# A two-layer transformer block on one Trainium2 core: the context's 192 features contracted as 128 rows and a rest of 64

## The chip, the core and the metric

The kernel is one program on one core of a Trainium2 chip. The core has five engines that run side by side and wait for each other through semaphores: TensorE (PE; its weight loads are listed apart as PEld), VectorE (DVE), ScalarE (ACT), GpSimd (POOL) and SyncE (SP), which here issues nearly all DMA transfers. TensorE's products land in PSUM, 128 partitions by eight banks of 512 fp32 columns; VectorE and ScalarE read them from there. The metric is the device time of one execution in microseconds, lower is better.

## What is computed

Two layers, each of self-attention, cross-attention to a context, and a gated feed-forward part, with a layer norm ahead of each and everything in fp32. x is (4, 512, 320): four batches of 512 tokens. The context is (4, 1601, 192). There are 20 heads of 16.

```python
def _attn(x, ctx, wq, wk, wv, wo, bo, heads):
    q = (x @ wq).reshape(b, n, heads, dh).transpose(0, 2, 1, 3)
    k = (ctx @ wk).reshape(b, j, heads, dh).transpose(0, 2, 1, 3)
    v = (ctx @ wv).reshape(b, j, heads, dh).transpose(0, 2, 1, 3)
    sim = jnp.einsum('bhid,bhjd->bhij', q, k) * scale
    a = jax.nn.softmax(sim, axis=-1)
    out = jnp.einsum('bhij,bhjd->bhid', a, v)
    return out.transpose(0, 2, 1, 3).reshape(b, n, heads * dh) @ wo + bo
...
x = _attn(h1, h1, q1, k1, v1, o1_w, o1_b, heads) + x
x = _attn(h2, context, q2, k2, v2, o2_w, o2_b, heads) + x
ff = a * jax.nn.gelu(g, approximate=False) @ ff_w2 + ff_b2
```

The change touches `ctx @ wk` and `ctx @ wv` of cross-attention: 192 features contracted, 1601 tokens, 320 columns, in each layer and batch.

## The kernel before

The program is a list of units. An attention unit is one layer, kind, batch and group of four heads (five groups, so 20 self-attention and 20 cross-attention units a layer); a feed-forward unit is one batch. The context's tokens are cut into 13 chunks of 128 (the last has 65).

**Rounds.** A cross unit runs 13 rounds, one for each chunk. In a round TensorE makes the scores of four heads (`st`, L1300: key times query in two parts, plus the row of maxima `nrows`), and beside them products of a coming unit from which its row maxima are taken (`sps`, L1068, and L1095 for the last 65 tokens). These run on four tiles of 32 rows by 128 columns. ScalarE turns `st` into exponentials `pr` (L1310), VectorE takes the maxima of `sps` (L1083). Then TensorE multiplies the exponentials of the chunk before with the values (`av`, L1326, tiles of 128 rows by 32 columns); ScalarE copies `av` out (L1345) and GpSimd adds it up (L1346). A self unit has 4 rounds of the same kind.

**Steps.** All other TensorE work of the attention stages is cut into steps that the scheduler puts between an `av` and the next round's scores: queries (`qps`, L941), output projections (`ops`, L1226), keys of the context (`kps`, L965, function `keys_of_context`) and values (`vps`, L1029, function `add_values`). Each step has an estimated cost and a due round; a credit that grows with the work still to be done says whether a round gets no step, one or more. The order is fixed when the program is built. A step takes a PSUM bank (of eight, chosen by the time at which each is expected to be free), writes it and has it copied out by VectorE or ScalarE, whichever is expected to be free first (`taken`, L1008 and L1011).

**The two steps that change.** The transposed context lies in a tile `[96, 2, tokens]`: 192 features as two times 96 partitions. A value step makes one chunk of 128 tokens for eight heads (128 columns) or twelve (192 columns): two contractions of 96 rows, each on four tiles of 128x32, one for each 32 tokens. There are 13 such steps for each of the two head sets. A key step makes 200 or 201 tokens of each half of the tokens for one unit, again in two contractions of 96 rows on four tiles; four steps make a unit's keys. Then GpSimd splits the keys into a high and a low part (`split`, L817 and L818), and SP moves them to the unit's key buffer `kT` (L866). Each fp32 product stands as two records in the trace.

**The context.** In layer 0, VectorE transposes it in blocks of 32, SP saves it to DRAM (L755), and loads it for each batch and layer in four bands for each of the two times 96 features (L769).

## Time and profile before

| what | time |
|---|---|
| three runs, median | 2946.81 us |
| three runs, lowest and highest | 2944.68 and 2947.46 us |
| the profiled execution's span | 2948.5 us |
| TensorE busy in it | 2871.7 us |
| VectorE busy | 2060.2 us |
| ScalarE busy | 1890.3 us |
| GpSimd busy | 1287.7 us |
| kps products, 2560 records (L965) | 330 to 541 ns each |
| vps products of cross-attention, 3264 records (L1029) | 270 to 350 ns each |

The profiled execution is a fourth one, with its own span. In the timeline a line has the start and the length in us, the engine, the source line, the operation, the tile written and those read, the shape, and how many instructions were merged; square brackets hold the idle time ahead of it and what ended it. A record's length is longer than the time after which the next one can begin, since products overlap; starts are the better measure. Group lines give busy time and the mean of one after the bar.

### The profile page before, as it was taken

What the parts mean: (1) busy time and instruction counts of PE and PEld (TensorE: products, weight loads), DVE (VectorE), ACT (ScalarE), POOL (GpSimd) and SP (SyncE); (2) the same over time, 40 slices, a digit from 0 to 9 for tenths busy, and PEclk for the clock granted to TensorE, in tenths of its full rate; (3) what the DMA queues carried; (4) which work ended last, traced back from release to release, by engine and by line L of the source; (5) the groups of instructions that cost most, each with busy time, mean ns of one, the idle gap of its engine ahead of it and who ended that gap; (6) DMA issues with size and microseconds to landing.
All of it is one profiled execution on the core that took longest, in us unless ns stands there. A gap on an engine that the chain in (4) does not pass through costs nothing.

```text
span 2948.5 us, 84388 instructions
## 1 busy us (share of the span) xinstructions
PE 2871.7 (97%) x35018; PEld 1513.0 (51%) x35018; DVE 2060.2 (70%) x4031; ACT 1890.3 (64%) x3754; POOL 1287.7 (44%) x1409
## 2 busy tenths in 40 slices
PE   8999999999999999999999999999999999999999
PEld 4555555555555554355554555555555555544554
DVE  7777888888888878323258678888888888873221
ACT  3867677887877878501138676778778788783000
POOL 3556345545545545211225563455455464451110
PEclk8999999999999999999999999999999999999999
DMA  4444224232232112200113342222221121222000
GB/s 106 107 124 101 69 67 108 52 89 59 50 93 68 47 50 62 83 18 11 42 40 89 100 101 68 64 62 54 54 65 47 50 72 45 58 53 78 20 22 14
DMA packets 186543, 188.70 MB, mean 64 GB/s; under 512 B 69668, under 2 KB 137264, under 8 KB 186160
## 3 DMA queue, kind: packets, MB, share of 16 engines
q1 hardware_dynamic: 185368, 182.11, 24.4%
q8 instruction: 276, 4.52, 0.6%
q10 hardware_dynamic: 760, 1.18, 0.2%
q14 instruction: 107, 0.88, 0.1%
q0 software_dynamic: 32, 0.00, 0.0%
HBM read 55.76 MB, written 29.36 MB: 29 GB/s over the span
## 4 chain that ended last, share of the span: by engine, by line
PE 81%; DVE 13%; ACT 1%; DMA 1%; issue 1%; POOL 1%; SPq 1%; POOLq 0%; ACTq 0%; DVEq 0%
PE av L1326 22%; PE st L1300 16%; PE fps L1411 10%; DVE pm L1083 8%; PE sps L1068 6%; PE yps L1518 6%; PE vps L1029 5%; PE ops L1226 3%; PE kps L965 3%; PE qkps L900 3%; DVE nmax L1083 3%; PE fps L1471 2%; PE qps L941 2%; PE sps L1095 1%; ACT pr L1310 1%
## 5 line engine op out<-in xcount | busy, mean ns | idle before, releaser
L1310 ACT ACTIVATE pr<-st 128x512 f32<-128x512 f32 (+1 forms) x2720 | 1404.4, 604 | 399.8 <-PE st L1300 364.9
L1083 DVE TENSOR_REDUCE pm<-sps 128x1 f32<-128x512 f32 x1920 | 1188.0, 681 | 147.7 <-PE sps L1068 139.0
L1346 POOL TENSOR_TENSOR o<-o,vo 128x512 f32<-128x512 f32 x576 | 739.2, 1283 | 960.8 <-ACT vo L1345 937.5
L1068 PE MATMUL sps<-kT,q 32*128 32x512 f32 x4800 | 867.5, 430 | 10.6 <-DMA q<-low 3.4
L1300 PE MATMUL st<-q,kT 32*128 32x512 f32 (+1 forms) x5120 | 782.4, 420 | 2.2 <-ACT low L916 1.7
L1326 PE MATMUL av<-pr,vals 128*32 128x512 f32 (+1 forms) x5440 | 736.8, 607 | 45.5 <-ACT pr L1310 10.0
L1300 PEld LDWEIGHTS st<-q,kT 32*128 32x128 f32 (+1 forms) x5120 | 417.2, 180 | 290.4 <-issue 120.4
L1300 PE MATMUL st<-nrows,ones 32*128 32x512 f32 (+1 forms) x2720 | 539.1, 399 | 9.4 <-DMA nrows<-turned 9.4
L1068 PEld LDWEIGHTS sps<-kT,q 32*128 32x128 f32 x4800 | 425.6, 184 | 91.1 <-ACT pr L1310 13.4
L1083 DVE TENSOR_REDUCE nmax<-sps 128x1 f32<-128x512 f32 x640 | 396.3, 681 | 103.6 <-PE sps L1068 96.0
L1345 ACT COPY vo<-av 128x512 f32<-128x512 f32 x576 | 354.1, 615 | 23.9 <-PE av L1326 20.1
L1482 ACT ACTIVATE gl<-fps,b 128x512 f32<-128x512 f32 x80 | 54.6, 687 | 414.4 <-PE fps L1471 303.2
L1411 PE MATMUL fps<-hT,w 128*128 128x512 f32 x640 | 283.0, 597 | 0.0
L1326 PEld LDWEIGHTS av<-pr,vals 128*32 128x32 f32 (+1 forms) x5440 | 111.1, 108 | 320.4 <-DVE pm L1083 182.1
L1300 PEld LDWEIGHTS st<-nrows,ones 32*128 32x128 f32 (+1 forms) x2720 | 245.1, 180 | 34.4 <-issue 8.4
L1483 DVE SCALAR_TENSOR_TENSOR hid<-fps,b,gl 128x512 f32<-128x512 f32 x80 | 59.6, 748 | 241.1 <-ACT gl L1482 239.1
L1411 PEld LDWEIGHTS fps<-hT,w 128*128 128x128 f32 x640 | 119.3, 190 | 155.3 <-issue 152.1
L1518 PE MATMUL yps<-w,hid 128*128 128x320 f32 x640 | 176.3, 435 | 0.1
L1518 PEld LDWEIGHTS yps<-w,hid 128*128 128x128 f32 x640 | 120.4, 190 | 56.5 <-ACT gl L1482 4.5
L1226 PEld LDWEIGHTS ops<-wo,aT 112*32 112x32 f32 (+1 forms) x3072 | 97.9, 110 | 57.9 <-issue 41.2
L1226 PE MATMUL ops<-wo,aT 112*32 112x160 f32 (+1 forms) x3072 | 124.1, 300 | 0.7 <-POOL aT L1208 0.6
L517 POOL TENSOR_SCALAR root<-root 128x4 f32<-128x4 f32 x22 | 5.2, 237 | 263.9 <-DVE root L511 263.2
(91 smaller groups left out, 2493.1 us busy)
## 6 DMA issues: line engine op xcount, KB each, us to landing
kT<-stages SPq DMA_DIRECT2D x160, 200.2 KB
oway<-o SPq DMA_DIRECT2D x80, 256.0 KB
q<-high SPq DMA_DIRECT2D x160, 64.0 KB
q<-low SPq DMA_DIRECT2D x160, 64.0 KB
kT<-high SPq DMA_DIRECT2D x60, 128.0 KB
q<-high SPq DMA_DIRECT2D x60, 128.0 KB
kT<-low SPq DMA_DIRECT2D x57, 128.0 KB
aT<-oway SPq DMA_DIRECT2D x32, 224.0 KB
```

What stands on the lines that cost most here:

```text
L900: nc.tensor.matmul(ps[f : f + m, :w], lhsT=wqk[:n, k, f // GD, column : column + m], rhs=first.hT[:n, k, at : at + w], start=(k == 0), sto ...
L1029: nc.tensor.matmul(ps[f : f + m, :w], lhsT=u.kvT[:n, k, at + f : at + f + m], rhs=wv[:n, k, h0 * DH : h1 * DH], start=(k == 0), stop=(k == ...
L1068: nc.tensor.matmul(ps, lhsT=u.q[j * SLOT : (j + 1) * SLOT, e, t * P : (t + 1) * P], rhs=u.kT[j * SLOT : (j + 1) * SLOT, u.k0 + s * 512 : u ...
L1083: nc.vector.tensor_reduce(to[:, j : j + 1], ps, AX.X, ALU.max)
L1226: nc.tensor.matmul(ps[f : f + m, : D // 2], lhsT=aT[:n, k, f * NQ + t * SLOT : f * NQ + t * SLOT + m], rhs=wo[:n, k, cols], start=(k == 0) ...
L1300: nc.tensor.matmul(own[0][:r, :], lhsT=ones[rows, :r] if e == 2 else u.keys(rows, c), rhs=u.rows[rows, :] if e == 2 else u.q[rows, e, :], ...
L1310: nc.scalar.activation(p[:r], own[0][:r], AF.Exp)
L1326: nc.tensor.matmul(ps[j * SLOT : (j + 1) * SLOT, :], lhsT=columns_of[:r, head : head + SLOT], rhs=pr.pop((c, j))[:r, :], start=True, stop= ...
L1345: nc.scalar.copy(vo, ps)
L1346: nc.gpsimd.tensor_tensor(u.o, u.o, vo, ALU.add)
L1411: nc.tensor.matmul(ps, lhsT=w1[:, k, i * FF + c * P : i * FF + (c + 1) * P], rhs=natural(u.hT[:, k]), start=start, stop=stop,)
L1518: nc.tensor.matmul(ps[:, :D], lhsT=hid[c][:, t * P : (t + 1) * P], rhs=w2[:, c, :], start=(c == 0), stop=(c == NHC - 1),)
```

## The change

Features 0 to 127 become one contraction of 128 rows; the remaining 64 a second one. Two such rests, of different tokens, lie side by side in one tile: one on partitions 0 to 63, the other on 64 to 127 (`RESTS`; the weights' rest is loaded twice, once for each half). A value step now makes two chunks that are three apart (`PAIRS`; the thirteenth alone) into two banks: main rows of the one, main rows of the other, then both rests on tiles of 64x32. A key step makes two cuts of the tokens into two banks in the same way, so two steps make a unit's keys. The token halves become 768 and 834 long; 66 tokens' products are made twice so that both halves of a bank have one width. The high part of the keys moves into the tile `w1`. The context's last 65 tokens are saved apart, and the context is loaded in five bands for the main rows and five for the rests. Estimated costs and due rounds of the steps follow. What follows the products (copies, split, moves) is otherwise the same.

```diff
 DK = [(0, 0, 112), (1, 112, 112), (2, 224, 96)]
 HK = [(0, 0, P), (1, P, 96), (2, P + 96, 96)]
-CK = [(0, 0, 96), (1, 96, 96)]
...
 KB = CTX // 32
-RUN = NC2 * 32
+KM = P // 32
+CR = CTX - P
 TOK = S2 + 1
-HALF = TOK // 2
-WIDTHS = [RUN - 32 + max(0, min(32, S2 - (NC2 - 1) * P - 32 * i)) for i in range(4)]
-WIDTHS[3] += TOK - S2
-BANDS = [(sum(WIDTHS[:i]), w) for i, w in enumerate(WIDTHS)]
+RUN = (NC2 - 1) * 32
+TAIL = TOK - 4 * RUN
+HALF = 2 * RUN
+LONG = HALF + TAIL
+
+
+RESTS = [(0, 0), (CR, 0), (0, RUN), (CR, RUN), (CR, 2 * RUN)]
+CROSS_W = TOK + RUN * 2 + TAIL
+QC = RUN // P
+PAIRS = [(c, c + QC) for h in range(2) for c in range(2 * h * QC, (2 * h + 1) * QC)] + [(NC2 - 1,)]
+STEP_OF = {c: i for i, pair in enumerate(PAIRS) for c in pair}
 KW = NC2 * P
 NHC = FF // P
...
-KCUT = slices(HALF, 4)
+KCUT = list(zip(slices(RUN, 2), ((RUN, RUN // 2), (RUN + RUN // 2, RUN // 2 + TAIL))))
...
-        room["low"], room["high"] = part(HALF), part(HALF)
+        room["low"] = part(LONG)
+        room["high"] = w1_flat[:, 2 * D + CROSS_W : 2 * D + CROSS_W + LONG]
...
         room["context"] = [
-            w1_flat[:96, 2 * D : 2 * D + 2 * TOK].rearrange("p (k w) -> p k w", k=2),
-            one.tile([96, 2, TOK], F32, tag="ctxT", name="ctxT"),
+            (t[:, :TOK], t[:, TOK:])
+            for t in (w1_flat[:, 2 * D : 2 * D + CROSS_W], one.tile([P, CROSS_W], F32, tag="ctxT", name="ctxT"))
...
-                lambda k=k: dma(out=t[:96, k], in_=w[k * 96 : (k + 1) * 96, :].rearrange("(k d) c -> d k c", d=32))
-                for k in range(2)
+                lambda k=k, to=to, at=at, n=n: dma(
+                    out=t[to : to + n, k], in_=w[at : at + n, :].rearrange("(k d) c -> d k c", d=32)
+                )
+                for k, to, at, n in ((0, 0, 0, P), (1, 0, P, CR), (1, CR, P, CR))
...
-            dma(out=saved[b][:, :, c0 * 32 : (c0 + n) * 32], in_=s[i][:, :, : n * 32])
+            if c0 + n < NC2:
+                dma(out=saved[b][:, :, c0 * 32 : (c0 + n) * 32], in_=s[i][:, :, : n * 32])
...
+            for band in range((TAIL + 31) // 32):
+                w = min(32, TAIL - band * 32)
+                dma(out=tails[b][:, :, band * 32 : band * 32 + w], in_=s[i][band * 32 : (band + 1) * 32, :, :w])
...
-            for i, (at, w) in enumerate(BANDS):
-                dma(
-                    out=s["cT"][:, k, at : at + w],
-                    in_=saved[b][i * 32 : (i + 1) * 32, k * 3 : (k + 1) * 3, :w],
-                )
+            main, rest = s["cT"]
+            for i, (row, col) in enumerate(RESTS):
+                part = saved[b][i * 32 : (i + 1) * 32] if i < 4 else tails[b]
+                w = RUN if i < 4 else TAIL
+                if k == 0:
+                    dma(out=main[:, i * RUN : i * RUN + w], in_=part[:, :KM])
+                else:
+                    dma(out=rest[row : row + CR, col : col + w], in_=part[:, KM:])
...
         def keys_of_context(part):
 
-            at, w = KCUT[part]
-            ps = bank("kps")
-            written(0.1 + w * 4 * 2 / 2400, ps)
-            for k in range(2):
+            cuts = KCUT[part]
+            main, rest = first.kvT
+            pss = [bank("kps") for _ in cuts]
+            written(0.2 + (sum(w for _, w in cuts) + cuts[1][1]) * 4 / 2400, *pss)
+            for e, (at, w) in enumerate(cuts):
                 for i in range(2):
                     for f in range(GT):
                         nc.tensor.matmul(
-                            ps[(i * GT + f) * SLOT : (i * GT + f + 1) * SLOT, :w],
-                            lhsT=wk2[:, k, u.g * GD + f * SLOT : u.g * GD + (f + 1) * SLOT],
-                            rhs=first.kvT[:, k, i * HALF + at : i * HALF + at + w],
-                            start=(k == 0),
-                            stop=(k == 1),
+                            pss[e][(i * GT + f) * SLOT : (i * GT + f + 1) * SLOT, :w],
+                            lhsT=wk2[:, 0, u.g * GD + f * SLOT : u.g * GD + (f + 1) * SLOT],
+                            rhs=main[:, i * HALF + at : i * HALF + at + w],
+                            start=True,
+                            stop=False,
+                        )
+            for i in range(2):
+                for f in range(GT):
+                    for e, (at, w) in enumerate(cuts):
+                        rows = slice(e * CR, (e + 1) * CR)
+                        col = (i - e) * RUN + at
+                        nc.tensor.matmul(
+                            pss[e][(i * GT + f) * SLOT : (i * GT + f + 1) * SLOT, :w],
+                            lhsT=wk2[rows, 1, u.g * GD + f * SLOT : u.g * GD + (f + 1) * SLOT],
+                            rhs=rest[rows, col : col + w],
+                            start=False,
+                            stop=True,
                         )
             low, high = room["low"], room["high"]
-            taken(low[:, at : at + w], ps[:, :w], ps, 0.12 + w * 0.001)
+            for (at, w), ps in zip(cuts, pss):
+                taken(low[:, at : at + w], ps[:, :w], ps, 0.12 + w * 0.001)
             if part + 1 < len(KCUT):
                 return
             split(low, high)
 
             def half(i):
-                to = u.kT[:, i * HALF : (i + 1) * HALF]
-                return [(to[h::2], t[i * GD : (i + 1) * GD]) for h, t in enumerate((high, low))]
+                w = (HALF, LONG)[i]
+                to = u.kT[:, i * HALF : i * HALF + w]
+                return [(to[h::2], t[i * GD : (i + 1) * GD, :w]) for h, t in enumerate((high, low))]
...
-            for part, (_, w) in enumerate(KCUT):
+            for part, cuts in enumerate(KCUT):
                 add(
-                    chain, 0.05 + w * 8 / 2400, lambda part=part: keys_of_context(part),
-                    keys_due - 2 * (len(KCUT) - 1 - part), lambda part=part: part or keys_free(),
+                    chain, 0.15 + (sum(w for _, w in cuts) + cuts[1][1]) * 4 / 2400, lambda part=part: keys_of_context(part),
+                    keys_due - 4 * (len(KCUT) - 1 - part), lambda part=part: part or keys_free(),
                 )
...
+        def cross_values(i, step):
+
+            h0, h1 = PARTS[i]
+            w = (h1 - h0) * DH
+            cols = slice(h0 * DH, h1 * DH)
+            main, rest = u.kvT
+            chunks = PAIRS[step]
+            pss = [bank("vps") for _ in chunks]
+            written(0.2 + w * 4 * (1 + len(chunks)) / 2400, *pss)
+            for c, ps in zip(chunks, pss):
+                for f, m in tiles_of(u.row_count(c)):
+                    nc.tensor.matmul(
+                        ps[f : f + m, :w],
+                        lhsT=main[:, c * P + f : c * P + f + m],
+                        rhs=wv2[:, 0, cols],
+                        start=True,
+                        stop=False,
+                    )
+            for f, m in tiles_of(u.row_count(chunks[0])):
+                for c, ps in zip(chunks, pss):
+                    b = c // QC if c < NC2 - 1 else 4
+                    row, col = RESTS[b]
+                    at = col + (c % QC if b < 4 else 0) * P + f
+                    rows = slice(row, row + CR)
+                    nc.tensor.matmul(
+                        ps[f : f + m, :w],
+                        lhsT=rest[rows, at : at + m],
+                        rhs=wv2[rows, 1, cols],
+                        start=False,
+                        stop=True,
+                    )
+            for c, ps in zip(chunks, pss):
+                put(i, c, ps)
             u.vmade[i] += 1
...
-            for c in range(u.nch):
-                add(
-                    "values", 0.05 + w / 600 * len(parts_k), lambda i=i, c=c: values(i, c),
-                    units[u.i + g].start + 2 * c, lambda c=c, free=free: free(c),
-                )
+            for c in range(u.nv):
+                if u.cross:
+                    add(
+                        "values", 0.15 + w / 600 * (1 + len(PAIRS[c])), lambda i=i, c=c: cross_values(i, c),
+                        units[u.i + g].start + 2 * PAIRS[c][0], lambda c=c, free=free: free(PAIRS[c][-1]),
+                    )
+                else:
+                    add(
+                        "values", 0.05 + w / 600 * len(HK), lambda i=i, c=c: values(i, c),
+                        units[u.i + g].start + 2 * c, lambda c=c, free=free: free(c),
+                    )
...
-                until(lambda: units[u.i - u.g].vmade[u.g // 2] > c, "values")
+                until(lambda: units[u.i - u.g].vmade[u.g // 2] > (STEP_OF[c] if u.cross else c), "values")
```

Where the steps stand on TensorE. First a value step in the first layer's second batch, heads 0 to 7 (`vps`; `av` ends the round before, `nrows` and `ones` the scores before that). Before:

```order
L1300 MATMUL st<-nrows_98,ones 128x512 x2
L1068 MATMUL sps<-kT_134,q_102 128x512 x2
L1326 MATMUL av<-pr,vals 32x512 x4
L1029 MATMUL vps<-wv_115,ctxT 32x128 x8
L1300 MATMUL st<-q_104,kT_135 128x512 x2
```

With the change, one round without a step and the step behind it, from behind an `av`:

```order
L1381 MATMUL st<-q_104,kT_139 128x512 x2
L1149 MATMUL sps<-kT_138,q_102 128x512 x2
L1381 MATMUL st<-q_104,kT_139 128x512 x2
L1149 MATMUL sps<-kT_138,q_102 128x512 x2
L1381 MATMUL st<-nrows_98,ones 128x512 x2
L1381 MATMUL st<-q_104,kT_139 128x512 x4
L1149 MATMUL sps<-kT_138,q_102 128x512 x2
L1381 MATMUL st<-nrows_98,ones 128x512 x2
L1149 MATMUL sps<-kT_138,q_102 128x512 x2
L1407 MATMUL av<-pr,vals 32x512 x4
L1090 MATMUL vps<-wv_115,ctxT 32x128 x8
L1103 MATMUL vps<-wv_115,ctxT 32x128 x8
```

Eight products in one round became sixteen in every second round (L1090 the main rows, L1103 the rests); the round ahead, which held a step of its own, has none. Next a key step in the same layer's last batch, before:

```order
L1068 MATMUL sps<-kT_135,q_104 128x512 x2
L1326 MATMUL av<-pr,vals 32x512 x4
L965 MATMUL kps<-ctxT,w_116 32x200 x8
L1300 MATMUL st<-q_103,kT_101 128x512 x2
L1068 MATMUL sps<-kT_135,q_104 128x512 x2
```

With the change, the second of the unit's two key steps in the same round:

```order
L1407 MATMUL av<-pr,vals 32x512 x4
L989 MATMUL kps<-ctxT,w_116 32x192 x4
L989 MATMUL kps<-ctxT,w_116 32x258 x4
L1001 MATMUL kps<-ctxT,w_116 32x192
L1001 MATMUL kps<-ctxT,w_116 32x258
L1001 MATMUL kps<-ctxT,w_116 32x192
L1001 MATMUL kps<-ctxT,w_116 32x258
L1001 MATMUL kps<-ctxT,w_116 32x192
L1001 MATMUL kps<-ctxT,w_116 32x258
L1001 MATMUL kps<-ctxT,w_116 32x192
L1001 MATMUL kps<-ctxT,w_116 32x258
L1381 MATMUL st<-q_103,kT_101 128x512 x2
```

The step holds the main rows of both cuts (L989), then the rests in turn from the two row halves (L1001).

More of the change, by code (lines that the diff above doesn't have):

```diff
@@ L732 @@
     saved = [dram.tile([P, KB, RUN], F32, name=f"ctxT{b}") for b in range(B)]
+    tails = [dram.tile([32, KB, TAIL], F32, name=f"tail{b}") for b in range(B)]
     users = []
@@ L1014, in add_values, with put @@
     def add_values(u):
-        parts_k = CK if u.cross else HK
-        wv = wv2 if u.cross else wv1
+        def put(i, c, ps):
+            h0, h1 = PARTS[i]
+            w = (h1 - h0) * DH
+            r = u.row_count(c)
+            taken(vals[:r, c, h0:h1, 0:DH], ps[:r, :w].rearrange("p (h d) -> p h d", d=DH), ps, 0.12 + w * 0.001)
         def values(i, c):
```

27 lines of the change are left out of this document (17 added, 10 removed).

## The prediction

> **What bounds the kernel now.** I read the page's shares and chain first, then the busy time in stretches, then the operations of the two tiles that change, then single rounds in the timeline of TensorE.
>
> ```profile
> span 2948.5 us, 84388 instructions
> PE 2871.7 (97%) x35018; PEld 1513.0 (51%) x35018; DVE 2060.2 (70%) x4031; ACT 1890.3 (64%) x3754; POOL 1287.7 (44%) x1409
> PE 81%; DVE 13%; ACT 1%; DMA 1%; issue 1%; POOL 1%; SPq 1%; POOLq 0%; ACTq 0%; DVEq 0%
> PE av L1326 22%; PE st L1300 16%; PE fps L1411 10%; DVE pm L1083 8%; PE sps L1068 6%; PE yps L1518 6%; PE vps L1029 5%; PE ops L1226 3%; PE kps L965 3%; PE qkps L900 3%; DVE nmax L1083 3%; PE fps L1471 2%; PE qps L941 2%; PE sps L1095 1%; ACT pr L1310 1%
> ```
>
> TensorE is busy for 97% and holds 81% of the chain; VectorE's maxima (L1083) are the only other entry of weight. The two operations that change, vps and kps, hold 5% and 3%. The stretches of the two cross-attention stages, columns PE, PEld, DVE, ACT, POOL, granted clock, DMA:
>
> ```profile
> 430.00:1190.00 760.00, 740.66 (x10571) 393.45 (x10574) 637.42 (x1237) 611.11 (x1228) 401.29 (x389) 1.00 0.27 67
> 1888.00:2646.00 758.00, 738.52 (x10620) 391.29 (x10612) 631.94 (x1205) 612.66 (x1228) 402.21 (x389) 1.00 0.23 56
> ```
>
> There VectorE works 84% of the time (637.42 of 760) and ScalarE 80%: TensorE binds, with two engines close behind. How close shows in one window that holds three kinds of round (TensorE alone; a round runs from one av to the next):
>
> ```profile
> 745.15 1.07 PE L1326 MATMUL av<-pr,vals 128*32 128x512 f32 x8
> 746.04 1.48 PE L941 MATMUL qps<-hT,wq 128*32 128x256 f32 x24
> 748.97 1.06 PE L1326 MATMUL av<-pr,vals 128*32 128x512 f32 x8
> ...
> 751.70 1.07 PE L1326 MATMUL av<-pr,vals 128*32 128x512 f32 x8
> ...
> 754.23 1.06 PE L1326 MATMUL av<-pr,vals 128*32 128x512 f32 x8
> 755.11 0.87 PE L965 MATMUL kps<-w 96*32 96x201 f32 x16
> ...
> 757.44 1.06 PE L1326 MATMUL av<-pr,vals 128*32 128x512 f32 x8
> ```
>
> and another with a value step and a round without a step before it:
>
> ```profile
> 606.85 1.07 PE L1326 MATMUL av<-pr,vals 128*32 128x512 f32 x8
> ...
> 609.61 1.06 PE L1326 MATMUL av<-pr,vals 128*32 128x512 f32 x8
> 610.50 0.62 PE L1029 MATMUL vps<-wv,ctxT 96*32 96x128 f32 x16
> ...
> 612.58 1.06 PE L1326 MATMUL av<-pr,vals 128*32 128x512 f32 x8
> ```
>
> Four records run side by side on the four 32-column tiles, so 24 records of 256 are 6 waves, 1536 columns in a row; kps is 4 waves of 201 (804), vps 4 of 128 (512). Their rounds take 3.82, 3.21 and 2.97 us. Both differences give 0.83 ns a column (0.85 us/1024, 0.24 us/292), and what is left is 2.54 us in all three. So a round with a step costs **2.54 us plus 0.83 ns a column**, and a step has no fixed price of its own that could be saved. A round without a step does not cost 2.54: the three here take 2.76, 2.73 and 2.53. Why, VectorE's row shows:
>
> ```profile
> 748.23 5.01 DVE L1083 TENSOR_REDUCE pm<-sps 128x1 f32<-128x512 f32 x8 [1.34 <-PE sps L1068]
> 748.44 2.06 ACT L1310 ACTIVATE pr<-st 128x512 f32<-128x512 f32 x4 [0.47 <-PE st L1300]
> ```
>
> Eight maxima without a gap, 0.63 each: four of them are 2.5 us, a round. Banks come free at that rate, and TensorE waits for them where no step stands between.
>
> **What the change removes: streaming.** Values, per layer and batch: 13 steps of 4 waves at 128 and at 192 columns become 6 steps of 6 waves (two chunks of 2 waves on 128 rows, and 2 waves for both rests, if eight tiles run side by side) and one of 4: 40 waves in place of 52, that is 12 x 320 x 0.83 = 3.2 us, for 8 of them **-25.6 us**. Keys, per unit: 4 steps of 4 waves of 200 or 201 (3204 columns) become 2 x (192+192+192+258) = 1668 for the main rows and 2 x (192+258) = 900 for the rests, the wider of the two counting: 636 columns fewer, 0.53 us, for 40 units **-21.2 us**. The counts of the trace are those of this reckoning (two records a product):
>
> ```profile
> L965 PE MATMUL kps<-w x1280: 330/332/357, 213.8 to 2356.8; 96*32 96x200 f32 x138, 96*32 96x201 f32 x45
> L965 PE MATMUL kps<-ctxT,w x1280: 330/332/541, 510.8 to 2567.4; 96*32 96x200 f32 x138, 96*32 96x201 f32 x45
> L1029 PE MATMUL vps<-wv,w x1632: 270/310/350, 337.4 to 2394.7; 96*32 96x128 f32 x91, 96*32 96x192 f32 x91
> L1029 PE MATMUL vps<-wv,ctxT x1632: 270/300/350, 526.7 to 2606.7; 96*32 96x128 f32 x91, 96*32 96x192 f32 x91
> ```
>
> **What it adds: a change of the tile's shape in each step.** Main rows run on 128x32 tiles, rests on 64x32, the attention round on 32x128. Before, a step follows av in av's shape. The prices of a change that the trace has:
>
> ```profile
> 529.63 0.62 PE L1029 MATMUL vps<-wv,ctxT 96*32 96x128 f32 x16
> 530.18 0.50 PE L1300 MATMUL st<-q,kT 32*128 32x512 f32 x2
> ```
>
> ```profile
> 1242.76 3.70 PE L1471 MATMUL fps<-hT,w1r 64*128 64x512 f32 x16
> 1246.39 14.00 PE L1411 MATMUL fps<-hT,w 128*128 128x512 f32 x32
> ```
>
> ```profile
> L1326 PE MATMUL av<-pr,vals x5440: 592/616/1063, 53.4 to 2677.4; 128*32 128x512 f32 x183, 65*32 65x512 f32 x12
> ```
>
> From vps to st 0.55 us pass where 512 columns take 0.43: 0.12 until the first record of the new shape. The second fence has a change from 128 to 64 rows, as here: 8 waves of 512 take 3.41 of the 3.63, so 0.22, with a weight load of 128 columns in it. The av records, of 32 columns like ours, read 592 where the shape stands and 616 behind a change: 0.025. I take 0.12 + 0.025 = 0.14 (ours load 32 columns, so nearer the low end), between 0.12 and 0.22. The new program has 205 more such changes: 112 value steps, 80 key steps, 13 where a second step follows in the same round. **+28.7 us**, between 25 and 45. The Trainium skill's TensorEngine Tiling (Array Packing), Key Properties, states that a change of mode (not of the tile alone) drains TensorE, and lists 128x32 and 64x32 as two modes. The three rows agree that a change costs; were 128 to 64 rows at the same 32 columns free, the sum below would be 28.7 lower.
>
> **What it moves: steps out of rounds.** 208 + 160 steps become 112 + 80. The scheduler still has 676 attention rounds; in the built order 168 had no step, 299 have none now. Those that stand first in a row rise from 99 to 161 and cost 0.2 more than 2.54 each (2.76, 2.73): 62 x 0.2 = 12.4. A second one costs nothing (2.53); third ones, outside the two long rows at the ends of cross-attention that stay, rise from 1 to 20, taken as the first: 3.8. Together **+16 us**, between 0 (if the longer steps let VectorE catch up) and 131 x 0.2 = 26. This is how the smaller number of steps is paid for.
>
> **Two banks at once.** A doubled step needs a second bank while the round before is being emptied. That bank's last tenant is mostly the round's second maximum. By the row at 748.23 it is done at 748.23 + 2 x 0.63 = 749.49, and a step behind that av would begin 0.88 after it (746.04 less 745.15), at 749.85: 0.36 us of cover. It is gone where VectorE runs late by a copy:
>
> ```profile
> 756.10 0.37 DVE L1008 COPY stages<-kps 128x201 f32<-128x201 f32 x1
> ```
>
> So a step pays 0 to 0.37, and nearer 0, since that copy lies behind the maxima. I take 0.03 for 192 steps: **+5.8 us**. Eight tiles starting one after another are in this too. The Trainium skill's TensorE: Matmul & The Clock Gate, Part 3 (the mechanism of row and column tiling), gives about 4 ns a tile; by that, an estimate, four more tiles cost 16 ns a step, 3 us in all, and the sum would be 3 lower. [...]
>
> **At nothing.** The copies out of PSUM stay as many (one a chunk, four a unit). GpSimd's split grows from 801 to 834 columns:
>
> ```profile
> L818 POOL TENSOR_TENSOR stages<-stages 128x801 f32<-128x801 f32 x40 | 64.1, 1602 | 3.2
> L817 POOL CAST stages<-stages 128x801 fp32r<-128x801 f32 x40 | 34.1, 852 | 43.0 <-DVE stages L1008 19.4 <-ACT stages L1011 11.0 <-DVE pm L1083 9.1
> ```
>
> 4% of 98 us, on an engine 44% busy; uncovered it is 0.1 us a unit, 4 us. On SP's queue the context takes 10 transfers a batch in place of 8, the saved tail 3 in place of 1:
>
> ```profile
> 525.55 2.53 SPq L866 DMA_DIRECT2D kT<-stages  x4
> PE st L1300 <- DMA nrows<-turned: 9.4, 9, 2.4
> ```
>
> 0.63 an issue: the loads go out in 16 groups, each of five now in place of four, and hold back what stands behind them (the rows of maxima, nrows) by 0.63 more, 10 us if each were waited for; but nrows cost 9.4 us in nine waits of 80 units, so a small part of that. The key moves leave in the same rounds as before, one or two off. The high half now lies in w1, whose last columns load after those moves in SP's own order.
>
> **The sum.** -25.6 - 21.2 + 28.7 + 16 + 5.8 = +3.7 on the span of 2948.5: 2952.2. That execution stands 1.7 us over the median of the runs (2946.81), so the time is **2950 us**, 0.1% more. A measurement tells about 0.2%, 5.9 us, from no change: the forecast is that the change pays for itself and no more. Its own range, with the bounds on the changes of shape, is 2942 to 2958.
>
> **Rivals.** First, faster: the steps now outlast VectorE's backlog, so every round without a step runs at 2.53, a change costs its lowest, 0.12, and banks nothing. -46.8 + 24.6 = -22 us, 2925. For it: the 2.53 row. Against: the 2.73 round stands right behind the longest step of the window (1.48 us). Second, slower: the second bank is late in most doubled steps, by 0.15. 192 x 0.15 = 28.8 in place of 5.8: +26.7 us, 2973; it decides from 0.04 a step. For it: VectorE is at 84%, and the maxima follow without a gap. Against: the 0.36 of cover. Third, also slower: the change does not do what it says, and the rests of two row halves run in fours. The rests are 35840 + 36000 columns, 60 us; at half as much again to twice, +34 to +64, 2981 to 3010. Against: the fps rows pass 16 records of 512 in 3.63, eight waves of two row halves.
>
> **How the numbers follow.** Forecast 0.48, first rival 0.22, second 0.18, third 0.12. The forecast's own spread lies mostly within 0.2% (0.30 of its 0.48), with 0.14 above and 0.04 below; the first rival is faster (0.21), the others slower (0.16 and 0.12). That makes faster 0.25, same 0.33, slower 0.42. The range of 8 in 10 reaches half into the first rival and over the second: 2930 to 2975.
>
> **What would show it.** Rests as 64x32 records, 16 in a step, 2 waves apart by 0.11 or 0.16 us: eight tiles run. 0.14 between main and rest: the change's price. A value step of 128 in a round of 2.54 + 0.64 + 0.14 = 3.32, a key step in 2.54 + 0.96 + 0.14 = 3.64 or 2.54 + 1.18 + 0.14 = 3.86. Rounds without a step at 2.73 and 2.53. TensorE's idle time ahead of vps and kps ended by VectorE would show the second rival; a key or query that lands late (DMA ahead of sps or st) would be a cause that I have not priced.

## The result, and the profile after

The changed kernel takes 2968.15 us (median of four runs, 2965.80 to 2972.44) where the old one took 2946.13 beside it: a ratio of 1.0075, 95% interval 1.0060 to 1.0089. It is slower, by three quarters of a per cent. The forecast was 2950, no difference that can be told, with 0.42 for slower; the time lies inside the range of 2930 to 2975 and beside the second rival's 2973, but not for that rival's reason. The profiled execution has a span of 2964.8 us against 2948.5: +16.3 us have to be explained where the sum had +3.7. The runs differ by more, 22.0: the old kernel's profiled execution was long among its own (granted clock 0.993, the changed kernel's 0.995; the old kernel's later executions had spans of 2946 to 2949 us at 0.993, 2942 to 2947 at 0.995), so the two traces show 16.3 of the 22.0.

The page of the changed kernel, span, busy time and the chain of waits:

```profile
span 2964.8 us, 84430 instructions
PE 2891.3 (98%) x35018; PEld 1483.2 (50%) x35018; DVE 2041.0 (69%) x3964; ACT 1918.6 (65%) x3821; POOL 1303.4 (44%) x1409
PE 80%; DVE 10%; POOL 3%; issue 2%; DMA 2%; ACT 2%; SPq 1%; POOLq 0%; ACTq 0%; DVEq 0%
PE av L1407 21%; PE st L1381 16%; PE fps L1492 9%; PE sps L1149 8%; PE yps L1599 6%; DVE pm L1164 6%; PE ops L1307 3%; PE qkps L923 3%; DVE nmax L1164 3%; PE fps L1552 2%; PE vps L1090 2%; PE kps L989 2%; PE qps L964 2%; PE vps L1103 2%; PE vps L1069 1%
```

The value steps hold as much of the chain as before (2, 2 and 1% in L1090, L1103 and L1069, the last of them self-attention's, where L1029 held 5% for all), the main rows of the keys 2% where the keys held 3%. 67 instructions went from VectorE (4031 to 3964) to ScalarE (3754 to 3821): copies out of PSUM, since the two copies of a doubled step are given to one engine each. The busy time of the two cross-attention stages, columns as in the prediction:

```profile
430.00:1196.00 766.00, 749.71 (x10575) 380.83 (x10573) 629.06 (x1207) 626.26 (x1264) 405.80 (x387) 1.00 0.27 67
1896.00:2660.00 764.00, 747.99 (x10596) 381.77 (x10597) 624.04 (x1173) 626.19 (x1263) 408.71 (x389) 1.00 0.22 56
```

Each stage is some 6 us longer; VectorE and ScalarE are now level. A doubled value step of 128 columns in TensorE's timeline:

```profile
530.12 1.06 PE L1407 MATMUL av<-pr,vals 128*32 128x512 f32 x8
531.00 0.62 PE L1090 MATMUL vps<-wv,ctxT 128*32 128x128 f32 x16
531.55 0.45 PE L1103 MATMUL vps<-wv,ctxT 64*32 64x128 f32 x16
531.93 0.50 PE L1381 MATMUL st<-q,kT 32*128 32x512 f32 x2
```

The 16 records of the rests take 0.38 us to the next shape, two waves and a change: eight tiles of 64x32 do run side by side. The single records start 7 ns apart. From main rows to st 0.93 us pass: 6 waves of 128 columns are 0.64, the usual way from such a step to st 0.12, and 0.17 is left for the change of shape (0.14) and for eight tiles starting one after another (0.03). The split into these two is a reckoning, four more starts of 7 ns being the 0.03; the sum is the same in the 92 doubled value steps that st follows (0.29 less 0.125, median). The doubled steps' rounds have medians of 3.34 (values of 128 columns) and 3.68 and 3.89 us (keys), 0.02 to 0.04 above the forecast's 3.32, 3.64 and 3.86. Streaming and shape are as forecast. What TensorE's weight loads waited for (us in total, times, longest), before:

```profile
PEld av L1326 <- DVE pm L1083: 182.1, 370, 1.1
PEld st L1300 <- ACT pr L1310: 103.1, 142, 0.8
PEld st L1300 <- DVE pm L1083: 30.8, 78, 0.8
```

and in the changed kernel:

```profile
PEld st L1381 <- ACT pr L1391: 189.7, 235, 1.7
PEld av L1407 <- DVE pm L1164: 159.4, 348, 0.6
PEld st L1381 <- DVE pm L1164: 49.9, 118, 0.8
```

A load may be late without holding a product up, so these are not losses yet; but they say where to look: the first products of a round (st) now wait for a bank that ScalarE or VectorE has still to read.

Losses are told from rounds. For every attention round, from the first record of one av to that of the next, I took off 2.54 us (or what rounds with another number of products take undisturbed), 0.83 ns a column of its steps, 0.14 a change of shape and 0.027 for a start of eight tiles. What is left over, summed in us, for the kernels that the argument needs (rounds of 12 products, 6 to 8 us in each, are in the total only; "long" is over 0.4 us left in one round):

| kernel | rounds without a step | short ones | long ones | rounds with a step | total |
|---|---|---|---|---|---|
| before | 130 | 17.1 | 11: 11.6 | 41.5 | 77.6 |
| the change | 262 | 34.9 | 41: 35.9 | 29.9 | 108.3 |
| merge_only | 255 | 33.6 | 50: 42.6 | 37.5 | 121.3 |
| one_bank | 255 | 32.0 | 55: 44.8 | 40.4 | 124.7 |
| one_copy | 255 | 34.0 | 52: 43.4 | 34.7 | 119.6 |
| keys_in_one | 292 | 32.1 | 59: 44.3 | 31.7 | 115.3 |
| finer_keys | 92 | 13.0 | 9: 8.9 | 58.7 | 88.8 |
| after_light_act | 262 | 11.5 | 47: 38.5 | 31.2 | 87.1 |
| after_light_dve | 262 | 40.2 | 32: 27.6 | 13.7 | 89.1 |
| after_light_both | 262 | 13.9 | 32: 27.7 | 13.3 | 60.9 |
| before_light_both | 130 | 6.7 | 9: 10.8 | 3.5 | 26.7 |

For the change the sum closes: -46.8 for the columns, +28.7 for the shapes, 192 x 0.027 = 5.2 for the starts and 108.3 - 77.6 = 30.7 make +17.8, where the span grew by 16.3. (Of the 192 steps only 176 have eight tiles, the thirteenth chunks have four: 0.4 us less.) The loss lies in the rounds without a step (+42.1), a part of it comes back in those with one (-11.6).

A long one, all engines, the doubled key step ahead of it included (rows of the two rounds from 408.30 and 412.77):

```profile
408.73 0.83 PE L989 MATMUL kps<-w 128*32 128x192 f32 x16
...
409.49 0.56 PE L1001 MATMUL kps<-w 64*32 64x192 f32 x16
...
410.18 0.32 ACT L1049 COPY stages<-kps 128x192 f32<-128x192 f32 x1 [0.49 <-PE kps L1001]
410.19 0.36 DVE L1046 COPY stages<-kps 128x192 f32<-128x192 f32 x1 [0.78 <-issue]
...
410.76 6.67 DVE L1164 TENSOR_REDUCE pm<-sps 128x1 f32<-128x512 f32 x11 [0.21 <-PE sps L1149]
...
412.77 1.06 PE L1407 MATMUL av<-pr,vals 128*32 128x512 f32 x8
413.76 0.18 PEld L1381 LDWEIGHTS st<-q,kT 32*128 32x128 f32 x2 [0.84 <-DVE pm L1164]
...
414.49 0.39 PEld L1381 LDWEIGHTS st<-q,kT 32*128 32x128 f32 x4 [0.19 <-DVE pm L1164]
...
415.09 0.51 PEld L1149 LDWEIGHTS sps<-kT,q 32*128 32x128 f32 x2 [0.20 <-DVE pm L1164]
...
416.07 1.06 PE L1407 MATMUL av<-pr,vals 128*32 128x512 f32 x8
```

During the step VectorE has read what there was and stands idle (0.78 and 0.21 us around its copy); then come eleven maxima without a gap, 0.61 each, into the round behind the next. The round without a step takes 3.30 us, and its loads come when a maximum has read a bank. What VectorE lost in the step it has little room to make up in a round that takes it 4 x 0.61 = 2.4 us of 2.54. That this is why the round is long is a reading of these rows, not shown.

### The profile page after: what moved, and what is told of

The parts are those of the page before. It is cut to its first block, busy times and chain, and to the rows that moved or that the text cites. A ratio compares the mean times of both kernels' runs of the same rounds, so it can differ in the third digit from the quotient of the medians.

```text
span 2964.8 us, 84430 instructions
## 1 busy us (share of the span) xinstructions
PE 2891.3 (98%) x35018; PEld 1483.2 (50%) x35018; DVE 2041.0 (69%) x3964; ACT 1918.6 (65%) x3821; POOL 1303.4 (44%) x1409
## 4 chain that ended last, share of the span: by engine, by line
PE 80%; DVE 10%; POOL 3%; issue 2%; DMA 2%; ACT 2%; SPq 1%; POOLq 0%; ACTq 0%; DVEq 0%
PE av L1407 21%; PE st L1381 16%; PE fps L1492 9%; PE sps L1149 8%; PE yps L1599 6%; DVE pm L1164 6%; PE ops L1307 3%; PE qkps L923 3%; DVE nmax L1164 3%; PE fps L1552 2%; PE vps L1090 2%; PE kps L989 2%; PE qps L964 2%; PE vps L1103 2%; PE vps L1069 1%
## 5 line engine op out<-in xcount | busy, mean ns | idle before, releaser
L1149 PE MATMUL sps<-kT,q 32*128 32x512 f32 x4800 | 901.9, 433 | 14.4 <-DMA q<-low 2.7
L1381 PE MATMUL st<-q,kT 32*128 32x512 f32 (+1 forms) x5120 | 800.3, 422 | 3.0 <-ACT low L939 2.3
L1381 PEld LDWEIGHTS st<-q,kT 32*128 32x128 f32 (+1 forms) x5120 | 426.4, 180 | 373.6 <-ACT pr L1391 185.0
L1381 PE MATMUL st<-nrows,ones 32*128 32x512 f32 (+1 forms) x2720 | 548.2, 403 | 5.8 <-DMA nrows<-turned 5.8
L1149 PEld LDWEIGHTS sps<-kT,q 32*128 32x128 f32 x4800 | 437.2, 184 | 105.0 <-DVE pm L1164 16.3
L1307 PEld LDWEIGHTS ops<-wo,aT 112*32 112x32 f32 (+1 forms) x3072 | 97.7, 110 | 60.3 <-issue 42.1
L923 PE MATMUL qkps<-hT,wqk 96*32 96x256 f32 (+1 forms) x1920 | 117.7, 387 | 1.4 <-DVE nmax L1164 1.3
```

The lines of the kernel that those rows point to most:

```text
L923: nc.tensor.matmul(ps[f : f + m, :w], lhsT=wqk[:n, k, f // GD, column : column + m], rhs=first.hT[:n, k, at : at + w], start=(k == 0), sto ...
L1149: nc.tensor.matmul(ps, lhsT=u.q[j * SLOT : (j + 1) * SLOT, e, t * P : (t + 1) * P], rhs=u.kT[j * SLOT : (j + 1) * SLOT, u.k0 + s * 512 : u ...
L1307: nc.tensor.matmul(ps[f : f + m, : D // 2], lhsT=aT[:n, k, f * NQ + t * SLOT : f * NQ + t * SLOT + m], rhs=wo[:n, k, cols], start=(k == 0) ...
L1381: nc.tensor.matmul(own[0][:r, :], lhsT=ones[rows, :r] if e == 2 else u.keys(rows, c), rhs=u.rows[rows, :] if e == 2 else u.q[rows, e, :], ...
```

## The experiments

Twelve kernels in three sets; each set ran beside the old kernel, which took 2945.89, 2948.09 and 2948.33 us. Ratios are to that.

### First set: steps, copies, the split

**split_steps.** The change with each step cut in two, a bank held open between the halves:

```diff
-            pss = [bank("vps") for _ in chunks]
+            pss = half_made.setdefault((i, step), [])
+            pss.append(bank("vps"))
+            ends = e == len(chunks) - 1
...
+            if not ends:
+                return
             for f, m in tiles_of(u.row_count(chunks[0])):
...
-                    add(
+                    for e in range(len(PAIRS[c])):
+                        add(
```

> The changed kernel with each step cut in two: the main rows of the first chunk (or cut) in one round, its bank held open; the main rows of the second and both rests in a later one. Products, columns, copies and the new contraction are those of the change; only the number of steps goes back up (187 attention rounds without a step in the built order; 168 before the change, 299 with it), and the shape changes grow from 205 to 227 over the old kernel. Theory A (the loss is in the rounds left without a step, which are longer than 2.54 us because VectorE and ScalarE have a round's work of about that length and the copies of a doubled step fall into them): -46.8 streaming, 227 x 0.14 = +31.8, +5.2 for the stagger, 19 more empty rounds x 0.25 = +5: about 5 us below the old kernel, 2941, and some 27 below the change. Theory B (67 copies out of PSUM went from VectorE to ScalarE): 224 copies are still on ScalarE here, so it stays at 2965 to 2970. Theory C (a change of shape costs more than 0.14): it has more of them, so it is slower than the change, above 2968.

3072.06 us, ratio 1.0424 (1.0410 to 1.0439). Theory C's words, above 2968, cover it, but not its reason: 22 more changes of shape would have to cost 4.7 us each. No theory had the size. This row of its weight loads shows why, and the row of the change to compare it with:

```profile
PEld sps L1165 <- DVE pm L1180: 114.7, 196, 1.7
```

```profile
PEld sps L1149 <- DVE pm L1164: 17.4, 53, 0.5
```

A round fills eight banks; with one held for a whole round, a second maximum's product waits for the first to be read. So the experiment changed more than it meant to, and says nothing between A and B. If all of the 104 us above the change are put down to the held banks, at most 176 of them, one costs 0.6 us; the run changed the order of the rounds too, so this is an estimate.

**merge_only.** The old contraction, merged steps:

```diff
-KCUT = slices(HALF, 4)
+KCUT = slices(HALF, 4)
+KCUT = [KCUT[:2], KCUT[2:]]
...
+PAIRS = [(c, c + QC) for h in range(2) for c in range(2 * h * QC, (2 * h + 1) * QC)] + [(NC2 - 1,)]
...
-            ps = bank("vps")
+            chunks = PAIRS[step] if u.cross else (step,)
+            pss = [bank("vps") for _ in chunks]
```

> The old kernel with its steps merged and nothing else changed: two chunks' values, or two cuts' keys, in one step into two banks, contraction on 96 + 96 rows as before, no 64-row tiles, the same columns. 295 rounds without a step in place of 168. Theory A: 127/131 of the 31 us by which attention rounds of the change exceed 2.54 us + columns + shape changes: about +30, 2976. The forecast's own price for rounds without a step: +16, 2962. Theory B: 217 copies on ScalarE in place of 153, as in the change, so +20, 2967. Theory C: no new shape changes, so it stays at the old time, 2946, within 6.

2992.72 us, ratio 1.0158 (1.0144 to 1.0173): 47 us slower than the old kernel, with not one column or shape changed. Theory C falls, the forecast's price (+16) is a third of it, and theory A's 2976 is 17 us too low too: it has the sign and the place, not the size. The wait that the changed kernel's rows showed is all there:

```profile
PEld st L1312 <- ACT pr L1322: 183.5, 234, 0.8
PEld av L1338 <- DVE pm L1095: 160.2, 347, 1.0
PEld st L1312 <- DVE pm L1095: 46.3, 104, 0.8
```

So among merged kernels the new contraction is worth having: the change stands 25 us below merge_only, where -46.8 + 28.7 + 5.2 gives -13, and what is left over in the rounds (108.3 against 121.3) the other 13. Whether it would be worth having with single steps, no run here shows.

**copies_back.**

```diff
-        if expect["dve"] < expect["act"]:
+        if expect["dve"] < expect["act"] + 0.6:
```

> The change, with the planner's choice of the engine that copies values and keys out of PSUM leaned to VectorE by 0.6 us, so that VectorE has 274 of the 432 copies and ScalarE 158 (212 and 220 in the change; 279 and 153 before it). Order of the products unchanged. Theory B (ScalarE's 67 extra copies, 22 us of its time, hold back the exponentials and so TensorE): 20 us faster than the change, about 2948. Theory A: the backlog only moves to VectorE, which is busy for as long: within 6 us of the change, 2962 to 2974. Theory C: unchanged, 2968.

2974.09 us, ratio 1.0096 (1.0081 to 1.0110), 6 us above the change. Theory B (2948) falls: which engine copies is not it.

**high_at_home.**

```diff
-        room["high"] = w1_flat[:, 2 * D + CROSS_W : 2 * D + CROSS_W + LONG]
-        room["in"] = [part(2 * CTX).rearrange("p (c d) -> p c d", d=CTX) for _ in range(2)]
+        room["high"] = part(LONG)
+        room["in"] = [
+            w1_flat[:, 2 * D + CROSS_W + i * 2 * CTX : 2 * D + CROSS_W + (i + 1) * 2 * CTX].rearrange("p (c d) -> p c d", d=CTX)
+            for i in range(2)
+        ]
```

> The change, with the high half of the keys' split back in the shared tile where it was, and the staged context rows in its place in w1. GpSimd's subtraction of the keys took 1975 ns with 834 columns where 801 took 1602: 15 us over 40 units. Theory D (that subtraction holds back GpSimd's additions to o, so ScalarE's copies of av and the exponentials behind them): the subtraction returns to about 1668 ns and the time falls by 10 to 15 us, to about 2955. Theories A, B and C: within 5 us of the change, whatever the subtraction takes.

2966.81 us, ratio 1.0068 (1.0056 to 1.0081), within the change's runs. GpSimd's subtraction in the change and here (count, busy, mean ns of one, idle before):

```profile
L841 POOL TENSOR_TENSOR stages<-stages,w 128x834 f32<-128x834 f32 x40 | 79.0, 1975 | 3.2
```

```profile
L844 POOL TENSOR_TENSOR stages<-stages 128x834 f32<-128x834 f32 x40 | 66.5, 1663 | 3.2
```

The place of `high` made the subtraction 0.31 us longer, and the time does not care. Theory D falls.

### Second set: banks or rounds

**one_bank.**

```diff
-            pss = [bank("vps") for _ in chunks]
-            written(0.1 + w * 4 * len(parts_k) * len(chunks) / 2400, *pss)
-            for c, ps in zip(chunks, pss):
+            whole = bank("vps")
+            written(0.1 + w * 4 * len(parts_k) * len(chunks) / 2400, whole)
+            for e, c in enumerate(chunks):
+                ps = whole[:, e * w : (e + 1) * w]
```

> The merged steps alone (old contraction, as in merge_only, which took 2993), but both chunks' values, or both cuts' keys, go into one bank side by side (2 x 192 or 201 + 200 of its 512 columns) and leave it by two copies on one engine, so that no bank is read by two engines. Steps, columns and rounds without a step are those of merge_only (295). Theory A (what costs is the rounds left without a step, whatever the banks): stays at 2985 to 2995. Theory E (what costs is the second bank, which the attention's products miss for the rest of the round): most of the 47 us over the old kernel goes, 2950 to 2960.

2995.97 us, ratio 1.0168 (1.0154 to 1.0181). It is no faster than merge_only: the second bank costs nothing that can be seen, and theory E falls. This could only be asked of the merged old kernel. The Trainium skill's TensorEngine Tiling (Array Packing), Gotcha 1, states that row tiles must write to different banks, so the two rests of the change cannot share one; no run here tries it.

**one_copy.** As one_bank, the pair leaving by one copy:

```diff
-            for (at, w), ps in zip(cuts, pss):
-                taken(low[:, at : at + w], ps[:, :w], ps, 0.12 + w * 0.001)
+            w = sum(w for _, w in cuts)
+            taken(low[:, at0 : at0 + w], whole[:, :w], whole, 0.12 + w * 0.001)
```

> As one_bank, and the pair leaves its bank by one copy of 384, 256 or 401 columns: 256 copies in place of 432 (180 on VectorE, 76 on ScalarE). A copy of 201 columns took 0.37 us and one of 128 took 0.29, so one of 401 should take about 0.57 in place of 0.74: 176 x 0.17 = 30 us less work over the two engines. Theory A: the lumps stay, the lighter engines give back a part: 2970 to 2985. Theory E: 2945 to 2955.

2991.20 us, ratio 1.0148 (1.0135 to 1.0162): 5 us less than one_bank for 176 copies fewer, above what any theory gave. The copies of the pairs are not what the long rounds wait for.

**keys_in_one.** The change, a unit's keys in one step:

```diff
-KCUT = list(zip(slices(RUN, 2), ((RUN, RUN // 2), (RUN + RUN // 2, RUN // 2 + TAIL))))
+KCUT = [((0, RUN), (RUN, RUN + TAIL))]
```

> The change, with a unit's keys made in one step in place of two: cuts of 384 and 450 columns, still two banks, two copies in place of four. Same streaming, 48 shape changes fewer (-6.7 us) and 40 eight-tile staggers fewer (-1.1); rounds without a step 329 in place of 299; doubled steps 136 in place of 176. Theory A at 0.31 us a round without a step (30.7 us over 131 is 0.23; merge_only gives 44 over 127, 0.34): +9, so 2968 to 2972, no better than the change. Theory E at 47/176 = 0.27 us a doubled step: -11 -8, 2950.

2962.04 us, ratio 1.0047 (1.0034 to 1.0061): 6 us below the change. 48 changes of shape and 40 starts of eight tiles fewer are worth 8; the 30 more rounds without a step cost some of it back (76.4 us over all of them, 70.8 in the change). Neither theory had the time, A's 2968 to 2972 nor E's 2950. It is the best of the versions with the new contraction that leave nothing out, and still slower than the old kernel.

**finer_keys.** The other way, eight key steps a unit in the old kernel:

```diff
-KCUT = slices(HALF, 4)
+KCUT = slices(HALF, 8)
...
-                    keys_due - 2 * (len(KCUT) - 1 - part), lambda part=part: part or keys_free(),
+                    keys_due - 1 * (len(KCUT) - 1 - part), lambda part=part: part or keys_free(),
```

> The old kernel with a unit's keys made in eight steps of 100 columns in place of four of 200, due one round apart: same streaming, one bank a step, 160 copies more (of about 0.27 us in place of half of 0.37), 127 rounds without a step in place of 168. Theory A: 41 x 0.3 = -12 us, 2934, less what the copies give back. Theory E: no gain, and 160 more banks taken: 2946 to 2960.

2960.39 us, ratio 1.0045 (1.0032 to 1.0058), against A's 2934; it stands at the upper end of E's 2946 to 2960, though one_bank speaks against E's reason. The rounds without a step do give back 7 us (28.7 to 21.9), but those with a step lose 17 (41.5 to 58.7): a step of a third of a microsecond seems to leave its own round waiting. The 160 more copies on VectorE and ScalarE could do that as well, and no run parts the two. Theory A holds for merging and falls as a straight line: fewer, longer steps leave more rounds bare, and more and shorter ones did not help either.

### Third set: lighter engines

```diff
-                nc.scalar.copy(vo, ps)
-                nc.gpsimd.tensor_tensor(u.o, u.o, vo, ALU.add)
+                nc.scalar.copy(vo[:, : N // 2], ps[:, : N // 2])
+                o2 = u.o.rearrange("p (e n) -> p e n", e=2)
+                vo2 = vo[:, : N // 2].rearrange("p (e n) -> p e n", e=1).to_broadcast([P, 2, N // 2])
+                nc.gpsimd.tensor_tensor(o2, o2, vo2, ALU.add)
```

```diff
-                    nc.vector.tensor_reduce(to[:, j : j + 1], ps, AX.X, ALU.max)
+                    nc.vector.tensor_reduce(to[:, j : j + 1], ps[:, :448], AX.X, ALU.max)
```

The first edit makes **after_light_act**, the second **after_light_dve**, both together **after_light_both** and, on the old kernel, **before_light_both**.

> The change, with ScalarE's work in a round cut: its copy of av takes 256 of the 512 columns (GpSimd adds these to both halves of o, so its work stays; the sums of the other columns are left out). A round's work on ScalarE was four exponentials of 0.515 and a copy of 0.61, 2.67 us, longer than TensorE's 2.54 without a step; it becomes about 2.4. Theory F (rounds without a step wait for ScalarE, whose lead of 0.13 us a round and copies only the rounds with a step make up): most of the 71 us by which these rounds exceed 2.54 goes, 40 us or more, below 2930. Theory V (the forecast's: VectorE's four maxima, 2.5 us, set these rounds): 10 us at most, 2958 to 2968.

> The change, with VectorE's work cut in place of ScalarE's: each maximum is taken over 448 of the 512 columns (keys 448 to 511 of each 512 are left out of the maximum), 0.55 us in place of 0.62, about 0.28 a round. Theory V: 40 us or more faster, below 2930. Theory F: 10 us at most.

> The change with both cuts. If ScalarE and VectorE together make the excess of the rounds without a step, it falls from 71 to 15 us or less: about 2905. If something else does (GpSimd, a transfer, the clock), it stays above 2940.

> The old kernel with both cuts. Its rounds without a step exceed 2.54 by 29 us, so it gains 20 to 30: about 2920. If the loss of the change lies in these two engines, the change is now the faster of the two, by about the 13 us of -46.8 + 28.7 + 5.2; if it lies elsewhere, the change stays some 20 us behind.

Measured: 2947.10 (ratio 0.9996, 0.9986 to 1.0005), 2949.52 (1.0006, 0.9997 to 1.0015), 2917.74 (0.9896, 0.9882 to 0.9911) and 2896.73 (0.9827, 0.9812 to 0.9842). So the change gains 21 us by the one, 19 by the other and 50 by both: neither theory's 40 came. But the old kernel gains 52, twice what was expected of it, and the change stays 21 us behind: the turn that I expected did not come.

The table of rounds tells the two cuts apart. ScalarE's took its 21 us from the short rounds without a step (34.9 to 11.5) and left the long ones and the rounds with a step as they were (35.9 to 38.5, 29.9 to 31.2). VectorE's did not shorten the short ones at all (34.9 to 40.2); it took 8 from the long ones and 16 from the rounds with a step. The median of the plain rounds without a step, 2.72 us in the change, is 2.57 with ScalarE's cut and 2.77 with VectorE's. So the ordinary excess of a round without a step is ScalarE's, as theory F had it, at half of F's size; the long ones answer a little to VectorE. ScalarE's copy of av in the change and with its cut:

```profile
L1426 ACT COPY vo<-av 128x512 f32<-128x512 f32 x576 | 352.9, 613 | 33.9 <-PE av L1407 23.5 <-POOL o L1427 8.6
```

```profile
L1426 ACT COPY vo<-av 128x256 f32<-128x256 f32 x576 | 230.8, 401 | 34.8 <-PE av L1407 27.3 <-POOL o L1429 6.8
```

With both cuts the rounds without a step of the change gave up 29 us (70.8 to 41.6), those of the old kernel 11 (28.7 to 17.5). But rounds with a step also became shorter, below the 2.54 that I had taken for TensorE's own: the median of the old kernel's, less their columns, fell from 2.545 to 2.477. It has more of them (508 against 377), and gained 38 us there where the change gained 17. VectorE's row of the old kernel with the cut shows 66 ns less an instruction than the 681 of the whole maxima:

```profile
L1083 DVE TENSOR_REDUCE pm<-sps 128x1 f32<-128x448 f32 x1920 | 1061.7, 615 | 187.4 <-PE sps L1068 180.0 <-PE st L1300 5.0
```

## Why the prediction held in its range and failed in one term

**What bounds the kernel.** "TensorE binds, with two engines close behind" was too kind to TensorE. The slope (0.83 ns a column) was right; the 2.54 us are not TensorE's floor, since the changed kernel's rounds with a step fall by 0.07 us in the median when only VectorE's work is cut.

**Streaming, -25.6 and -21.2, and the changes of shape, +28.7.** Right, by the 0.93 us of the value step. The Trainium skill's TensorEngine Tiling (Array Packing), Key Properties, states that a change of mode drains TensorE and gives no price; the trace agrees that going from 128x32 to 64x32 is not free, at 0.14 us.

**Two banks at once, +5.8.** Right in size for another reason: 5.2 us are the eight tiles' starts, 27 ns a step. The Trainium skill's TensorE: Matmul & The Clock Gate, Part 3, gives about 4 ns a tile, from which the estimate was 16 ns a step; the trace differs, with single starts 7 ns apart. A late bank does not show as more waiting ahead of the steps. What the loads of kps waited for, before:

```profile
  ACT pr L1310: 12.9, 43
  DVE pm L1083: 3.7, 12
```

and in the changed kernel, in half as many steps:

```profile
  ACT pr L1391: 7.4, 24
  DVE pm L1164: 2.4, 8
```

The loads of vps, self-attention's included, waited 19 us for ScalarE and VectorE before and 21 now.

So the second rival, whose time is nearest to the result, did not happen as described, and one_bank shows the bank to be free of charge in the merged old kernel. The third fell with the sixteen records of 531.55.

**At nothing.** GpSimd's subtraction became 23% longer, not 4%; high_at_home shows that nothing hung on it. The longer run of transfers on SP did not make the rows of maxima later: TensorE waited 5.8 us for them in place of 9.4.

```profile
PE st L1381 <- DMA nrows<-turned: 5.8, 8, 1.9
```

**Steps out of rounds, +16: the step that failed.** It measured +42.1 in the rounds without a step, and -11.6 in those with one, +30.5 together. The prediction had it that a first round without a step costs 0.2 more than 2.54, a second one nothing (2.53), and a third 0.2, and that VectorE's four maxima, 2.5 us, are why. The short ones came out so in size (34.9 - 17.1 = +17.8), but VectorE was the wrong engine: they shrink when ScalarE's copy is cut and not when the maxima are. The reason stood in the prediction's own fence: the row at 748.44 has four exponentials in 2.06 us, and with a copy of av of 0.61 ScalarE's round is 2.67, longer than 2.54, where VectorE's 2.5 is not. What it left out in size are the long ones: 11 of 130 with 11.6 us were in the trace of before, and there are 41 of 262 with 35.9 now, +24.3 us; in 36 of these, with 28.4 us, every wait ended with VectorE or ScalarE reading a bank (before: 8, with 6.0). Second rounds in a row cost 0.26 on average, not nothing. Had I divided the 28.7 us of all 130 rounds by their number, 0.22, in place of reading three in one window, the term would have been 131 x 0.22 = 29, and the sum a span of 2965. That this is so near is in part luck: the rounds without a step lost 42.1, not 29, and a gain that I did not price, the 11.6 us less in the rounds that keep a step, makes up for it.

**The forecast's own range.** 2942 to 2958 does not follow from the bounds named: 25 and 45 in place of 28.7 give 2946 to 2966. The time lies above both. And a run's time is 1.8 us longer than its span (2966.61 and 2964.8 for the profiled one), so the old kernel's trace stood 3.5 us above its median run, not 1.7.

**What is shown and what is not.** Shown: merging the steps costs 47 us by itself, with the order that the planner then chooses; in the merged old kernel not by the second bank and not by the number of the copies, in the changed kernel not by the engine of the copies and not by GpSimd; the loss lies in the rounds left without a step (28.7 us before, 76.2 in merge_only); the short excess of these rounds is ScalarE's. Argued from rows like those of 410.19 and 410.76, not shown: that in the long rounds the engines have run dry in a longer step and cannot make it up in a round that fills them; VectorE's cut took 8 of their 36 us, ScalarE's none. Open: what part the order of the banks has. The planner gives a product the bank that it expects free first, and its estimates know nothing of the new rounds. I set the bank of each product, as the program was built, beside the ends of the reads in the trace, and took the time by which a product's bank came free after both the bank free earliest and the start of the record ahead of it. That is about 29 us in the changed kernel (old kernel 17, merge_only 35, one_bank 27), 8 of it in the long rounds; the earlier bank would then be missing elsewhere. By this rough measure the order may account for up to 12 us of the 16.3, and it is not the whole of the long rounds. A planner with measured durations was not tried, nor the new contraction in single steps. No version here that leaves nothing out beats the old kernel.

## What to carry to other kernels

Work that is spread in small pieces between the rounds of a pipeline is also the time in which the other engines catch up; gathering it into fewer pieces saved nothing on the engine that does it and left bare rounds behind, here 47 us for 176 pairs, 0.27 each. Price such rounds by the mean over all that the trace has, the long ones included, not by the few of a clean window, and add up each engine's work in a round before naming the one that sets it. And a floor read from a trace (2.54 us) is a floor only once a cut of the other engines' work leaves it standing.

## What was not expected of the hardware

Eight fp32 tiles of 64x32 ran side by side at full rate, for 27 ns a step. A PSUM bank kept open from one round into a later one cost up to 0.6 us, an estimate from split_steps. GpSimd's subtraction of 834 columns took 1663 ns with both operands in one tile and 1975 with one of them in `w1`. The maxima took 0.61 us each without a gap, and 64 columns fewer made an instruction 66 ns shorter.
